# Two graph layers: the second layer's sent rows are loaded and halved in four of five pieces during the update of the last nodes

## The chip, the cores and the metric

The kernel runs on one core of a Trainium2 chip. The metric is the device time of one execution in microseconds (us), as the median of the runs; a profiled execution has a time of its own and a span, from its first to its last instruction. The core has five engines with a queue each: TensorE (PE, with PEld for loading its stationary operand), VectorE (DVE), ScalarE (ACT), GpSimd (POOL) and SyncE (SP), which issues most of the DMAs.

## The reference, cut to what matters

There are 3125 nodes of 256 numbers and 53125 directed edges. Four layers follow each other, each added to `x` behind a layer norm: an edge network with a node update, a mixture of four experts, a graph layer of two mean aggregations, and a feed-forward layer for the nodes with the highest weights. The graph layer is the one that matters here:

```python
def _sage_conv(x, src, tgt, W_l, b_l, W_r):
    msgs = x[src]
    agg = jax.ops.segment_sum(msgs, tgt, num_segments=n)
    deg = jax.ops.segment_sum(jnp.ones((src.shape[0],), x.dtype), tgt, num_segments=n)
    agg = agg / jnp.maximum(deg, 1.0)[:, None]
    return agg @ W_l + b_l + x @ W_r
h = jax.nn.relu(_sage_conv(x, src, tgt, W_l1, b1, W_r1))
logits = _sage_conv(h, src, tgt, W_l2, b2, W_r2)
```

## The kernel before, in words

The nodes are cut into 25 blocks of 128 (`NB`), and the blocks go through the node updates in pairs: block 24 alone first, then 0 and 1, up to 22 and 23.

*Dealing and edges.* The kernel first sorts the edges by source into buckets. The edge stage (`edges_by_bucket`, L776) then walks over 25 groups of buckets with five rounds each. POOL gathers rows of a table by indirect DMA (L807), VectorE adds (L845), ScalarE takes the relu (L850), and TensorE sums by source (L856). For each group it also counts the edges between every two nodes with one-hot matrices (L873 to L909) and writes the counts to `adj_h` in DRAM as f16. These tiles lie in the pool `bk`; `degs` and `hsb` of `close` (L859) hold what the group hands to the node update.

*Node updates.* They are generators that are advanced in small pieces between the steps of the edge stage. `first_part` is `update` (L583) and a layer norm; `second_part` is `experts` (L682), another layer norm and `sends` (L737). `update` loads `ux` on SyncE (L586), adds it to a matmul's result on VectorE (L619), and ends in L628. `experts` has two `sh` activations (L689 through `dense`, L579), four small expert networks (L709, L711), weights by L698 and L699, and adds the result to `x` at L734. `sends` writes a row block `zt` to `zres` in DRAM: its first half is what a node sends (times W_l1), its second what it keeps (times W_r1, plus the bias). The update tiles lie in the pool `upd`. All matmul results of the updates take turns in three PSUM banks (`ring(es, 3)`, L780).

When the last group is done, `all_pieces()` is called twice (L1015, L1016): the first call runs `first_part` of blocks 22 and 23 together with `second_part` of blocks 20 and 21 to their end, the second runs `second_part` of blocks 22 and 23.

*The graph layer.* `sums_of_few` (L1299) keeps the sent rows of all nodes on chip as `z1`, in two halves: the value rounded to the fast matmul type, and the rest. `halve` (L1307) makes them, the first on ScalarE (L1310), the second on VectorE (L1311). For each block of targets, `fetch` (L1315) loads the counts of two blocks as `two` (1600 KB), `widen` (L1324) turns one block of it into `slab`, its first nine parts on VectorE (L1328) and the other sixteen on ScalarE (L1329), `count` (L1332) adds up the degrees on VectorE, and 25 matmuls (L1402) sum into `padj`. The second sweep does the same with `z2`. The order of the work before the first sweep:

```python
fetch(0)
for k0 in range(0, NB, 5):
    v = z1[:, k0:k0 + 5, D:].bitcast(F32)
    nc.sync.dma_start(v, zres[k0 * P:(k0 + 5) * P, :D].rearrange("(k p) d -> p k d", p=P))
    if k0 == 0:
        widen(0)
        fetch(1), fetch(2)
    halve(z1, k0, v)
count(0)
```

A fetch of an odd block does nothing, since its pair is there already. Each engine works through its queue strictly in order. Within a stage that order is the one in which the kernel is written (a manual schedule), engine by engine, but the framework may draw work of a following stage forward where its inputs and its place in memory come free early. Before the change it does so with the first `two`, which stands behind `ux` and ahead of the last four stores of `zt`, and with slab 0, which is made among the L619 of blocks 22 and 23. The framework puts the tiles of pools into memory like a stack, from the left, or from the right where a pool says so, and makes the first user of a place wait for the last user of what lay there. The loads of the second layer's weights (`lr2`, L1191, and `b2`, L1192) and POOL's adds of `b2` to `x` (L1236) were drawn forward too, into the edge stage, one pair of adds with each pair of blocks.

Of the kernel before, what the change touches and what calls it, by code (L numbers as in the profile page):

```python
# [8 lines left out]
F32 = mybir.dt.float32  # L9
F16 = mybir.dt.float16  # L10
F32R = mybir.dt.float32r
I32 = mybir.dt.int32
AF = mybir.ActivationFunctionType
OP = mybir.AluOpType
AX = mybir.AxisListType

P = 128
N, E, D, HID = 3125, 53125, 256, 512
NB = -(-N // P)
# [31 lines left out]
def gnn_ffn_kernel(ctx: ExitStack, tc: tile.TileContext, a: dict, out: bass.AP):  # L51
    nc = tc.nc
# [6 lines left out]
    def ring(stack, bufs=8):  # L59
        rings.append(stack.enter_context(tc.tile_pool(name="psum", bufs=bufs, space=bass.MemoryType.PSUM)))  # L60
# [26 lines left out]
    def load(pool, name, shape, src, eng=None):  # L87
        t = pool.tile(shape, F32, name=name)
        (eng or queue[0]).dma_start(t, src)
        return t  # L90
# [7 lines left out]
    def row_bias(pool, name, b, n):  # L98
        return load(pool, name, [P, n], bass.AP(tensor=b.tensor, offset=b.offset, ap=[[0, P], [1, n]]))
# [57 lines left out]
    zres = dram.tile([NP, 2 * D], F32, name="zres")  # L157
# [4 lines left out]
    first = ExitStack()  # L162
# [353 lines left out]
    def rest_of(fast):  # L516

        rs, l0 = ExitStack(), ExitStack()
# [62 lines left out]
        st = {}  # L581
# [177 lines left out]
        def first_part(group, sums, got):  # L759

            yield from update(*group, sums)
            got.append((yield from normal(group, "xT1")))

        def second_part(group, got):

            yield from experts(*group, got[0])
            xT = yield from normal(group, "xT2")
            yield from sends(*group, xT)

        def finish_nodes(group, sums):  # L770
# [2 lines left out]
            yield  # L773
            yield from second_part(group, got)

        def edges_by_bucket():  # L776
            with tc.tile_pool(name="bk", bufs=2) as bp, tc.tile_pool(name="upd", bufs=2) as up, \
                    tc.tile_pool(name="pA", bufs=2, space=bass.MemoryType.PSUM) as pA, \
                    tc.tile_pool(name="pH", bufs=1, space=bass.MemoryType.PSUM) as pH, ExitStack() as es:
                ring(es, 3)  # L780
                st["up"] = up

# [138 lines left out]
                def pieces(n=1):  # L921
                    for _ in range(n):
                        next(parts[turn[0] > 2 and turn[0] % 2], None)
                        turn[0] += 1

                def all_pieces(pair=None, of=()):

                    pieces(99)
                    parts[1] = second_part(*going.pop()) if going else iter(())
                    parts[0] = iter(())  # L930
                    if pair:
                        got = []
                        parts[0] = first_part(pair, of, got)
                        going.append((pair, got))
                    turn[0] = 0


                def take(it, n=1):
                    for _ in range(n):
                        next(it, None)  # L940

                def step(i):
                    g, r = steps[i]
                    return units[g], r
# [14 lines left out]
                for hf, w in ((half0, W0), (half1, W1)):  # L959
                    left = NP - NBK * BN  # L960
# [17 lines left out]
                for i, (g, r) in enumerate(steps):  # L978
                    u, more = units[g], i + 1 < len(steps)
                    coming = []  # L980
                    if more:
                        v = step(i + 1)
# [25 lines left out]
                    if r == ROUNDS - 1:  # L1008
                        take(tally, 99)
                        tally = counts(units.pop(g))  # L1010
                        if g % UB == UB - 1 or g == order[0]:
                            k0 = g - g % UB
                            all_pieces((k0, g - k0 + 1), [sums.pop(k) for k in range(k0, g + 1)])
                take(tally, 99)
                all_pieces()  # L1015
                all_pieces()  # L1016
            rings.pop()

# [149 lines left out]
        if fast:  # L1168
            edges_by_bucket()
        else:  # L1170
            with ExitStack() as es:
                ring(es)
                with tc.tile_pool(name="keys", bufs=1) as kp:
                    edges_by_scatter(kp)
                st["up"] = es.enter_context(tc.tile_pool(name="upd", bufs=2))
                for k0, nb in PAIRS:
                    got = []
                    for k in range(k0, k0 + nb):
                        hs = st["up"].tile([P, HW], F32, name="h0")
                        nc.sync.dma_start(hs, hsum[k * P:(k + 1) * P, :])  # L1180
                        got.append((hs, None))
                    for _ in finish_nodes((k0, nb), got):
                        pass
            rings.pop()
        ring(rs)


        wl1 = rs.enter_context(tc.tile_pool(name="wl1", bufs=1, side="right"))
        lr2 = wl1.tile([P, 2, 2 * D], F32, name="lr2")
        for j, w in enumerate("lr"):  # L1190
            nc.sync.dma_start(lr2[:, :, j * D:(j + 1) * D], a[f"L1_gnn_W_{w}2"].rearrange("(k p) m -> p k m", p=P))  # L1191
        b2 = row_bias(wl1, "b2", a["L1_gnn_b2"], D)  # L1192
        l0.close()


        left, right = ExitStack(), ExitStack()
        cp = left.enter_context(tc.tile_pool(name="conv", bufs=1))
        slp = left.enter_context(tc.tile_pool(name="slab", bufs=2))
        rdeg = cp.tile([P, NB], F32, name="rdeg")
# [2 lines left out]
        def side_of(k):  # L1202
            return (half0, K0, k) if k < K0 else (half1, NB, k - K0)
# [95 lines left out]
        def sums_of_few():  # L1299
# [1 line left out]


            z2 = cp.tile([P, NB, 2 * D], F32R, name="z2")
            zp = right.enter_context(tc.tile_pool(name="z1p", bufs=2, side="right"))
            z1 = zp.tile([P, NB, 2 * D], F32R, name="z1", bufs=1)

            def halve(z, k, v):  # L1307

                first, rest = z[:, k:k + v.shape[1], :D], z[:, k:k + v.shape[1], D:]
                nc.scalar.activation(first, v, AF.Copy)  # L1310
                nc.vector.tensor_tensor(rest, v, first.bitcast(F32), op=OP.subtract)  # L1311

            pairs, slabs = {}, {}

            def fetch(k):  # L1315

                rows, end, o = side_of(k)
                if o % 2 == 0:
                    n = min(2, end - k) * P
                    two = slp.tile([P, NB, 2 * P], F16, name="two")  # L1320
                    nc.sync.dma_start(two[:, :, :n], rows[:, o * P:o * P + n].rearrange("(k p) c -> p k c", p=P))
                    pairs[k] = pairs[k + 1] = two, n

            def widen(k):  # L1324
                o = side_of(k)[2] % 2 * P
                slab = slp.tile([P, NB, P], F32R, name="slab")
                two = pairs[k][0]
                nc.vector.tensor_copy(slab[:, :9], two[:, :9, o:o + P])  # L1328
                nc.scalar.activation(slab[:, 9:], two[:, 9:, o:o + P], AF.Copy)  # L1329
                slabs[k] = slab  # L1330

            def count(k):  # L1332

                two, n = pairs[k]
                if side_of(k)[2] % 2:
                    return
                m = slp.tile([P, 12, 2 * P], F16, name="m12", bufs=1)
                with nc.allow_low_precision("whole numbers below 2048"):
                    nc.vector.tensor_tensor(m[:, :, :n], two[:, :12, :n], two[:, 12:24, :n], op=OP.add)
                    for w in (6, 3):  # L1340
                        nc.vector.tensor_tensor(m[:, :w, :n], m[:, :w, :n], m[:, w:2 * w, :n], op=OP.add)
                    nc.vector.tensor_tensor(m[:, 0, :n], m[:, 0, :n], m[:, 1, :n], op=OP.add)
                    nc.vector.tensor_tensor(m[:, 2, :n], m[:, 2, :n], two[:, 24, :n], op=OP.add)
                    deg = slp.tile([P, 2 * P], F16, name="degs")
                    nc.vector.tensor_tensor(deg[:, :n], m[:, 0, :n], m[:, 2, :n], op=OP.add)
                degs[k] = degs[k + 1] = deg
# [6 lines left out]

            degs = {}
            fetch(0)
            for k0 in range(0, NB, 5):
                v = z1[:, k0:k0 + 5, D:].bitcast(F32)
                nc.sync.dma_start(v, zres[k0 * P:(k0 + 5) * P, :D].rearrange("(k p) d -> p k d", p=P))  # L1358
                if k0 == 0:
                    widen(0)  # L1360
                    fetch(1), fetch(2)
                halve(z1, k0, v)
            count(0)

            todo = {}
# [1 line left out]
            for i in range(2 * NB + 1):  # L1367
                k, second = i % NB, i >= NB
# [38 lines left out]
        if fast:  # L1407
            with tc.manual_schedule():
                sums_of_few()
        else:  # L1410
            sums_of_any()
# [4 lines left out]
        with tc.tile_pool(name="ffn", bufs=2) as fp, tc.tile_pool(name="rank", bufs=1) as rp:  # L1416
# [8 lines left out]
            for k in range(NB):  # L1425
                w = wcol[:, k:k + 1]
# [13 lines left out]
            for k0, nb in GROUPS:  # L1440
# [5 lines left out]
                for i in range(nb):  # L1446
                    k = k0 + i
# [18 lines left out]
    with tc.If(ok > 0) as cmp:  # L1466
        rest_of(True)
    with cmp.Else():
        rest_of(False)
# [38 lines left out]
```

## Time and profile before

| | us |
|---|---|
| median of 3 runs | 2130.91 (2130.25 to 2131.38) |
| the profiled execution's own time | 2126.99 |
| its span | 2125.1 |

The span falls into stages, with TensorE's busy share of each from the trace:

| stage | from, to (us) | TensorE busy |
|---|---|---|
| dealing | 0 to 470 | 62% |
| edges, with the updates of blocks 24 and 0 to 21 | 470 to 1505 | 78% |
| rest of the updates of blocks 20 to 23 | 1505 to 1567 | 88% |
| from the last `zt` to the second block of the first sweep | 1567 to 1595 | 35% |
| first sweep | 1595 to 1791 | 100% |
| second sweep | 1791 to 1938 | 98% |
| last layer | 1938 to 2125 | 95% |

How to read a profile line: start and duration in us (of a group of equal instructions, merged), the engine, the line of the kernel, the operation, the tile written `<-` the tiles read, the shape, and in brackets how long the engine was idle before it and what released it. `SPq` is the queue of SyncE, which issues DMAs; its durations are those of issuing, not of the transfer. In the chain, a DMA's duration goes from its issue to its landing. The granted clock (`PEclk`) is the share of TensorE's full clock that was granted.

### The profile page before, as it was taken

What the parts mean: (1) busy time and instruction counts of PE and PEld (TensorE: products, weight loads), DVE (VectorE), ACT (ScalarE), POOL (GpSimd) and SP (SyncE); (2) the same over time, 40 slices, a digit from 0 to 9 for tenths busy, and PEclk for the clock granted to TensorE, in tenths of its full rate; (3) what the DMA queues carried; (4) which work ended last, traced back from release to release, by engine and by line L of the source; (5) the groups of instructions that cost most, each with busy time, mean ns of one, the idle gap of its engine ahead of it and who ended that gap; (6) DMA issues with size and microseconds to landing.
All of it is one profiled execution on the core that took longest, in us unless ns stands there. A gap on an engine that the chain in (4) does not pass through costs nothing. (4 is left out here: it accounts for less than half of the span.)

```text
span 2125.1 us, 25417 instructions
## 1 busy us (share of the span) xinstructions
PE 1681.3 (79%) x7515; PEld 1031.4 (49%) x7515; DVE 1488.9 (70%) x4174; ACT 942.0 (44%) x1695; POOL 983.9 (46%) x1044
## 2 busy tenths in 40 slices
PE   3666676661067898898899889889859999999998
PEld 1333232320034555465555555555537777886666
DVE  6888888883047878777777877778437675667960
ACT  1222222220047767666666676667333333443222
POOL 3677777777757655655565565564000000111011
PEclk9777777775579999999999999999989999999999
DMA  8332332321199777777776767774235545550010
GB/s 298 113 107 97 107 115 88 127 96 32 40 308 284 200 220 216 206 200 225 208 204 211 207 194 218 209 219 140 71 117 126 136 115 148 137 152 1 0 40 23
DMA packets 238444, 316.49 MB, mean 149 GB/s; under 512 B 34458, under 2 KB 168968, under 8 KB 237928
## 3 DMA queue, kind: packets, MB, share of 16 engines
q1 hardware_dynamic: 182216, 164.43, 25.8%
q0 software_dynamic: 52512, 142.96, 23.3%
q10 hardware_dynamic: 3568, 7.38, 1.0%
q8 instruction: 62, 1.02, 0.2%
q14 instruction: 86, 0.70, 0.1%
HBM read 229.71 MB, written 84.96 MB: 148 GB/s over the span
## 5 line engine op out<-in xcount | busy, mean ns | idle before, releaser
L807 POOL DMA_INDIRECT cb<-tab_b,goes_to x490 | 472.8, 965 | 372.7 <-issue 109.0
L438 POOL DMA_INDIRECT cbuf<-rt,to x416 | 410.5, 987 | 166.1 <-issue 99.8
L845 DVE TENSOR_TENSOR cb<-pa,cb 128x1024 f32<-128x1024 f32 x245 | 288.5, 1216 | 99.9 <-PE pa L840 64.3
L1402 PE MATMUL padj<-z,slab 128*128 128x512 f32 x1250 | 321.0, 409 | 15.9 <-DVE z L1311 15.8
L850 ACT ACTIVATE cb<-cb 128x1024 f32<-128x1024 f32 x245 | 254.8, 1051 | 56.5 <-DVE cb L845 55.8
L1402 PEld LDWEIGHTS padj<-z,slab 128*128 128x128 f32 x1250 | 232.2, 191 | 75.0 <-issue 23.0
L107 ACT ACTIVATE oT<-pt 64x512 fp32r<-64x512 f32 (+1 forms) x250 | 145.1, 580 | 176.8 <-PE pt L826 173.8
L900 PE MATMUL pn<-ob,oa 128*128 128x448 f16 (+1 forms) x692 | 160.3, 349 | 47.6 <-ACT cn L107 35.2
L130 POOL TENSOR_TENSOR x<-x,xn 128x256 f32<-128x256 f32 x25 | 24.5, 982 | 352.1 <-DVE xn L127 352.1
L840 PE MATMUL pa<-gives,oT 128*128 128x512 f32 x490 | 166.4, 462 | 21.9 <-ACT oT L107 10.2
L885 DVE TENSOR_SCALAR ob<-ids,rows 128x448 f16<-128x448 f16 (+1 forms) x490 | 165.0, 337 | 0.0
L881 DVE TENSOR_SCALAR oa<-ids,rows 128x128 f16<-128x128 f16 x692 | 164.9, 265 | 0.0
L343 PE MATMUL pp<-mw,xTa 128*128 128x512 f32 x200 | 138.6, 848 | 10.3 <-ACT xTa L107 10.3
L107 ACT ACTIVATE cn<-pn 128x352 f16<-128x352 f32 x196 | 97.3, 496 | 99.3 <-PE pn L900 88.9
L856 PE MATMUL ph<-cb,rows 128*32 128x512 f32 x980 | 140.1, 621 | 1.2 <-ACT cb L850 1.1
L900 PEld LDWEIGHTS <-oa 128*128 128x128 f16 x692 | 62.1, 99 | 160.2 <-issue 112.0
L331 PE MATMUL pt<-ident,xn 128*128 128x128 f32 x50 | 16.8, 438 | 133.8 <-DVE xn L326 133.8
L840 PEld LDWEIGHTS pa<-gives,oT 128*128 128x128 f32 x490 | 95.7, 205 | 53.5 <-ACT oT L107 14.9
L826 PE MATMUL pt<-ident_r,rows 128*64 128x128 f32 x490 | 52.4, 231 | 84.7 <-DMA rows<-cbuf 84.7
L1329 ACT ACTIVATE slab<-two 128x2048 fp32r<-128x2048 f16 x50 | 95.6, 1911 | 39.6 <-PE padj L1402 38.8
L107 ACT ACTIVATE total<-pk 1x98 f16<-1x98 f32 x103 | 24.5, 238 | 178.9 <-PE pk L404 178.8
L826 PEld LDWEIGHTS pt<-ident_r,rows 128*64 128x64 f32 x490 | 51.4, 143 | 104.5 <-issue 87.4
(242 smaller groups left out, 3029.5 us busy)
## 6 DMA issues: line engine op xcount, KB each, us to landing
two<-adj_h SPq DMA_DIRECT2D x24, 1600.0 KB
rows<-cbuf SPq DMA_DIRECT2D x25, 680.0 KB
gives<-tab_h SPq DMA_DIRECT2D x48, 256.0 KB
adj_h<-cn SPq DMA_DIRECT2D x100, 112.0 KB
adj_h<-cn SPq DMA_DIRECT2D x100, 88.0 KB
cb<-tab_b,goes_to POOLq DMA_INDIRECT x490, 4.3
cbuf<-rt,to POOLq DMA_INDIRECT x416, 2.2
cbuf<-empty ACTq DMA_DIRECT2D x4, 1632.0 KB
```

Source lines behind the costliest of these rows:

```text
L107: nc.scalar.activation(dst, src, AF.Copy)
L343: nc.tensor.matmul(pp, lhsT=xT[:, c, :], rhs=mw1[:, 2 * h + c, :], start=c == 0, stop=c == 1)
L438: one_of = nc.gpsimd.indirect_dma_start(out=cbuf[:], out_offset=bass.IndirectOffsetOnAxis(ap=to[:n, i:i + 1], axis=0), in_=rt[:n, i, :], i ...
L807: nc.gpsimd.indirect_dma_start(out=cb[:, j, :], out_offset=None, in_=tab_b[:], in_offset=bass.IndirectOffsetOnAxis(ap=u["to"][:, i:i + 1], ...
L840: nc.tensor.matmul(got[j // 2][:, j % 2, :], lhsT=oT[:, j, :], rhs=u["ag"][:, j, :], start=True, stop=True)
L845: nc.vector.tensor_tensor(cb[:, j:j + 2], pa, cb[:, j:j + 2], op=OP.add)
L850: nc.scalar.activation(h, h, AF.Relu)
L856: nc.tensor.matmul(u["ph"][j * BN:(j + 1) * BN, :], lhsT=u["rows"][:, GB * r + j, :BN].bitcast(F32), rhs=hs[j // 2][:, j % 2, :], start=r ...
L881: nc.vector.tensor_scalar(oa, ids[:, 1 + i * P:1 + (i + 1) * P], field[:, 0:1], None, op0=OP.is_equal)
L885: nc.vector.tensor_scalar(ob[:, :w], ids[:, 1:w + 1], field[:, 1:2], None, op0=OP.is_equal)
L900: nc.tensor.matmul(pn[:, :w], lhsT=u["oa"].pop((j, r, i)), rhs=u["ob"][j, r][:, :w], start=r == rs[0], stop=r == rs[-1])
L1402: nc.tensor.matmul(pa, lhsT=slab[:, c, :], rhs=(z2 if second else z1)[:, c, :], start=c == 0, stop=c == NB - 1)
```

## The change

Pool `bk` is opened after `upd` and closed when the last group's counts are done, ahead of the last two calls of `all_pieces`. At that place the weights of the second layer are loaded (`second_weights`), `z1` is placed, and four of its five pieces are loaded: the sent rows of blocks 0 to 19. After the first `all_pieces()`, `second_part` of the last pair is advanced in fives, and one of the four pieces is halved after each five. The fifth piece, blocks 20 to 24, is loaded and halved where all five were before. `halve` itself is the same, moved to an outer function.

```diff
--- before.py
+++ after.py
@@ -773,10 +773,27 @@
             yield
             yield from second_part(group, got)
 
+        right = ExitStack()
+
+        def halve(z, k, v):
+
+            first, rest = z[:, k:k + v.shape[1], :D], z[:, k:k + v.shape[1], D:]
+            nc.scalar.activation(first, v, AF.Copy)
+            nc.vector.tensor_tensor(rest, v, first.bitcast(F32), op=OP.subtract)
+
+        def second_weights():
+            wl1 = rs.enter_context(tc.tile_pool(name="wl1", bufs=1, side="right"))
+            st["lr2"] = lr2 = wl1.tile([P, 2, 2 * D], F32, name="lr2")
+            for j, w in enumerate("lr"):
+                nc.sync.dma_start(lr2[:, :, j * D:(j + 1) * D],
+                                  a[f"L1_gnn_W_{w}2"].rearrange("(k p) m -> p k m", p=P))
+            st["b2"] = row_bias(wl1, "b2", a["L1_gnn_b2"], D)
+
         def edges_by_bucket():
-            with tc.tile_pool(name="bk", bufs=2) as bp, tc.tile_pool(name="upd", bufs=2) as up, \
+            with tc.tile_pool(name="upd", bufs=2) as up, ExitStack() as of_edges, \
                     tc.tile_pool(name="pA", bufs=2, space=bass.MemoryType.PSUM) as pA, \
                     tc.tile_pool(name="pH", bufs=1, space=bass.MemoryType.PSUM) as pH, ExitStack() as es:
+                bp = of_edges.enter_context(tc.tile_pool(name="bk", bufs=2))
                 ring(es, 3)
                 st["up"] = up
 
@@ -1012,7 +1029,17 @@
                             k0 = g - g % UB
                             all_pieces((k0, g - k0 + 1), [sums.pop(k) for k in range(k0, g + 1)])
                 take(tally, 99)
+                of_edges.close()
+                second_weights()
+                st["z1"] = z1 = right.enter_context(tc.tile_pool(name="z1p", bufs=1, side="right")).tile(
+                    [P, NB, 2 * D], F32R, name="z1")
+                for k0 in range(0, NB - 5, 5):
+                    nc.sync.dma_start(z1[:, k0:k0 + 5, D:].bitcast(F32),
+                                      zres[k0 * P:(k0 + 5) * P, :D].rearrange("(k p) d -> p k d", p=P))
                 all_pieces()
+                for k0 in range(0, NB - 5, 5):
+                    pieces(5)
+                    halve(z1, k0, z1[:, k0:k0 + 5, D:].bitcast(F32))
                 all_pieces()
             rings.pop()
 
@@ -1185,15 +1212,13 @@
         ring(rs)
 
 
-        wl1 = rs.enter_context(tc.tile_pool(name="wl1", bufs=1, side="right"))
-        lr2 = wl1.tile([P, 2, 2 * D], F32, name="lr2")
-        for j, w in enumerate("lr"):
-            nc.sync.dma_start(lr2[:, :, j * D:(j + 1) * D], a[f"L1_gnn_W_{w}2"].rearrange("(k p) m -> p k m", p=P))
-        b2 = row_bias(wl1, "b2", a["L1_gnn_b2"], D)
+        if not fast:
+            second_weights()
+        lr2, b2 = st["lr2"], st["b2"]
         l0.close()
 
 
-        left, right = ExitStack(), ExitStack()
+        left = ExitStack()
         cp = left.enter_context(tc.tile_pool(name="conv", bufs=1))
         slp = left.enter_context(tc.tile_pool(name="slab", bufs=2))
         rdeg = cp.tile([P, NB], F32, name="rdeg")
@@ -1301,14 +1326,7 @@
 
 
             z2 = cp.tile([P, NB, 2 * D], F32R, name="z2")
-            zp = right.enter_context(tc.tile_pool(name="z1p", bufs=2, side="right"))
-            z1 = zp.tile([P, NB, 2 * D], F32R, name="z1", bufs=1)
-
-            def halve(z, k, v):
-
-                first, rest = z[:, k:k + v.shape[1], :D], z[:, k:k + v.shape[1], D:]
-                nc.scalar.activation(first, v, AF.Copy)
-                nc.vector.tensor_tensor(rest, v, first.bitcast(F32), op=OP.subtract)
+            z1 = st["z1"]
 
             pairs, slabs = {}, {}
 
@@ -1353,13 +1371,11 @@
 
             degs = {}
             fetch(0)
-            for k0 in range(0, NB, 5):
-                v = z1[:, k0:k0 + 5, D:].bitcast(F32)
-                nc.sync.dma_start(v, zres[k0 * P:(k0 + 5) * P, :D].rearrange("(k p) d -> p k d", p=P))
-                if k0 == 0:
-                    widen(0)
-                    fetch(1), fetch(2)
-                halve(z1, k0, v)
+            v = z1[:, NB - 5:, D:].bitcast(F32)
+            nc.sync.dma_start(v, zres[(NB - 5) * P:, :D].rearrange("(k p) d -> p k d", p=P))
+            widen(0)
+            fetch(1), fetch(2)
+            halve(z1, NB - 5, v)
             count(0)
 
             todo = {}
```

In the resulting order of the engines' queues, SyncE issues the three loads of weights and the four pieces ahead of `ux` of blocks 22 and 23 (L586), and the first `two` after the last store of `zt`. On ScalarE and VectorE the four halvings stand among the instructions of `experts` for blocks 22 and 23. TensorE's order is the same. POOL's first twenty adds of `b2` stand together behind the last gathers.

## The prediction

> **What bounds the kernel now.** I first read the page's chain of work that ended last. From 1595.08 us on it is TensorE nearly without a break (L1402, L1232, then the last layer), so whatever moves the start of that stretch moves the end by as much. The chain over 1500 to 1600 us shows what sets that start (start, us, what):
>
> ```profile
> 1566.55 0.43 DVE zt L745
> ...
> 1567.00 2.03 DMA zres<-zt
> ...
> 1577.50 9.35 DMA z<-zres
> ...
> 1586.87 1.28 ACT z L1310
> ...
> 1588.17 1.49 DVE z L1311
> 1589.66 1.68 DVE m L1339
> ...
> 1593.76 1.27 DVE slab L1328
> ...
> 1595.08 4.30 PE padj L1402 x12
> ```
>
> The last zt row is ready at Z = 1566.98; block 1 of the first sweep starts 28.1 us later. Of these, 21.2 go until the fifth piece of z1 is on VectorE (1588.17), and 6.9 to its halving, `count` and the copy of slab 1. This end is what the change attacks. The SyncE queue says why the pieces come late (start, us, engine, line):
>
> ```profile
> 1505.09 1.28 SPq L586 DMA_DIRECT2D ux<-own  x1
> 1512.54 0.38 SPq L1321 DMA_DIRECT2D two<-adj_h  x1
> 1540.99 26.33 SPq L747 DMA_DIRECT2D zres<-zt  x4
> 1569.19 0.37 SPq L1358 DMA_DIRECT2D z<-zres  x1
> 1569.61 0.52 SPq L1321 DMA_DIRECT2D two<-adj_h  x1
> 1570.18 8.84 SPq L1358 DMA_DIRECT2D z<-zres  x4
> ```
>
> It serves in order: ux, the first `two`, four stores, and only then five pieces, with a second 1600 KB `two` between them. ScalarE took the pieces up at 1573.47, 1581.22, 1583.10, 1584.97 and 1586.87: one after the other, 1.9 us each for 640 KB, at 345 to 351 GB/s.
>
> The third view is the ux consumer in the node updates. These are VectorE's and TensorE's lines:
>
> ```profile
> 1513.26 0.42 DVE L619 TENSOR_TENSOR uT<-pd,ux 128x256 f32<-128x256 f32 x1 [0.79 <-PE pd L618]
> ```
> ```profile
> 1515.65 1.03 PE L578 MATMUL pd<-xT,ew 128*128 128x256 f32 x4
> ...
> 1522.42 1.78 PE L628 MATMUL pupd<-uw,uT 128*128 128x256 f32 x7 [0.57 <-DVE uT L619]
> ```
>
> ux was issued at 1505.09 and never waited for. The matmuls at 1515.65 need the PSUM bank that this first L619 frees (ring of three). Last, the granted clock (window, length, busy us, clock, DMA share, GB/s) falls when TensorE idles:
>
> ```profile
> 1585.00:1587.00 2.00, 2.00 (x6) 1.52 (x5) 1.62 (x2) 1.38 (x2) 0.00 (x0) 0.50 0.82 260
> 1587.00:1589.00 2.00, 2.00 (x8) 1.58 (x8) 1.60 (x2) 2.00 (x2) 0.00 (x0) 0.85 0.00 0
> ...
> 1595.00:1597.00 2.00, 1.92 (x6) 1.53 (x6) 1.80 (x7) 1.91 (x1) 0.00 (x0) 0.50 0.28 44
> ```
>
> **Part 1, the four early pieces: a new wait for ux.** In the changed program's order SyncE issues lr2 (two), b2, four pieces, and only then ux. The first piece lies over the edge tiles (cb, hsb, degs, oa, ob), so it waits for the last reader of degs, the second L611 pair, as the first `two` does today: issue at 1512.54, not 1505. ux waits for nothing itself, but stands behind it. Data flowed at full rate about 1.9 us after an issue (`two` at 1512.54: 190 GB/s by 1514 to 1515, 338 after). Four pieces and ux are 4x0.655 + 0.524 = 3.15 MB; at 348 GB/s 9.0 us, so ux lands at 1512.54 + 1.9 + 9.0 + 0.4 = 1523.9. L619 goes from 1513.26 to 1523.9. VectorE holds everything behind it (all L619, L699, L630, the norms), TensorE stops before the matmuls of 1515.65 and ScalarE behind both. They resume at 1523.9 + 0.45 = 1524.35.
>
> From there TensorE's queue up to L628 is 6.2 us of work (1515.65 to 1521.85), at first at half clock: TensorE has stood 8.7 us. In the row above it got its full clock back 3.3 us after it became busy at 1584.07, so about 1.6 us are lost. L628 starts at 1524.35 + 6.2 + 1.6 = 1532.15 instead of 1522.42: **+9.75**. (Before lost 0.57 there, since slab 0's copy stood ahead of the last L619; that goes.) Bounds: ux not queued behind the data would land at about 1516.2 + 4 = 1520.2 (today some 4 us from issue to last byte), -3.7; at the 290 GB/s of `two` it comes 1.9 later.
>
> **Part 2, the four halvings in the last pair's experts.** Each is 1.27 us ScalarE and 1.49 VectorE; the pieces have landed 20 us before. The order gives their places. The first ScalarE copy stands ahead of the two `sh` activations at 1544.48: `sh` comes 1.35 later, TensorE's next matmuls 1.2. The second and third stand ahead of L711, where ScalarE idled 0.74 each: they add 0.2 or less. The fourth follows the last L711, in a 5 us idle. On VectorE the first three fit the waits ahead of both L699 (3.77 and 2.61 idle); the fourth stands between L734 and the statistics at 1558.00, on the path: 1.45. Sum 1.45 + 1.45 = **+2.9**; 0 if all hide, 4x(1.27 + 1.49) = 11.0 if none does. With 0.1 for a colder clock at L742, Z moves by 9.75 + 2.9 + 0.1 = **+12.75**.
>
> **Part 3, from Z to block 1.** The first `two` no longer goes early: it now lies over the update tiles, zt among them, and stands behind the fourth store. Issue at Z + 2.05 (store) + 0.15 = Z + 2.2; landing, by its row (1512.54 to 1520.56), 8.0 later, Z + 10.2. The fifth piece follows it by 1.9, Z + 12.1. ScalarE copies its part of slab 0 (1.91 from Z + 10.25), then halves (1.27); VectorE takes the fifth piece at Z + 13.5 instead of Z + 21.2: **-7.7**. The 6.9 us behind it stay. Block 0 hides: its first nine matmuls need only VectorE's part (Z + 11.6), 22 of them take some 7 us with the cold start, and `degs` comes at Z + 19.1. TensorE is then busy shortly before block 1, whose first twelve matmuls took 4.30 at the clock of 0.50 above; warm, at the 3.58 for fifteen of the later blocks, 2.87: **-1.4**. The second `two` and res come 5.8 + 0.9 after the fifth piece, Z + 18.8, and are needed at Z + 20.9: hidden by 2 us; without cover it is their lateness.
>
> A rule would make this sum otherwise. The Trainium skill, "DMA: Bandwidth & Descriptors", "Anatomy of one DMA", gives a fit of about 2.0 us plus bytes/436e3 (for the software path; SBUF side). By it ux lands after 2.0 + 7.2 us, 2.1 sooner, and `two` after 5.8 instead of 8.0: the total below would be about -1. The rows of this very queue are 348 and 290 GB/s; I take them.
>
> **Part 4, what costs nothing.** lr2 and b2 leave the middle of the edge stage, and 18 of POOL's adds of b2 (L1236) with them: each pair was followed by 2.5 to 4.4 us of idle POOL until ScalarE's hsb, so a shorter burst releases no gather; that stage is 88% TensorE. Bound: the one VectorE wait for a gather after 816 us, 3.0. The 20 adds (0.74 each) then run from about 1508 to 1524, ahead of POOL's L728, needed at 1542. The other edits rename or reorder pools.
>
> **Sum.** +12.75 - 7.7 - 1.4 = +3.65, say +3.7. Against the profiled execution's 2126.99 us (span 2125.1) that is 2130.7; the median of the runs is 2130.91, so I predict **2134.6**. A difference within 0.2% (4.3 us) is about what a measurement of this kernel can't tell from none.
>
> **Rivals.**
> - *ux is not held up* (the engines share it with the pieces, or the pieces go earlier). For it: 16 engines. Against: today's pieces landed strictly one after another. Then +9.75 goes: 2130.9 + 2.9 + 0.1 - 9.1 = 2124.8, faster. Half held, at 1520.2: about 2131.
> - *The halvings hold the expert chain*, slower: each of ScalarE's four copies delays an activation that TensorE waits for, 4x1.27 + 1.49 = 6.6 instead of 2.9: 2138.3. It decides once L628 to the last zt grows by over 5 us. For: strict order, short idles (0.74). Against: the three idles above.
> - *The change doesn't do what it says*: pieces that land after their halving. They land by 1522, the first halving comes at about 1554; 2% at most.
>
> **Chances.** Mine, 2132 to 2137.5: 55%. The halvings, late pieces or a longer ux wait: 27%. Partly or not held up: 18%, the smaller part of it below 2126.6. The upper part of my own case is beyond +4.3. So faster 0.11, same 0.41, slower 0.48; range 2127 to 2139.5.
>
> **What would show it.** ux landing near 1524 with an L619 that waits for DMA, and a TensorE hole of 8 to 9 us from 1515.6; a clock of 0.50 behind it; the last zt near 1580; the first `two` issued 2.2 behind it; block 1 near 1600 at full clock. If L619 doesn't wait, the first step is wrong and the kernel is faster; if Z comes after 1583, the second is.

## The result and the profile after

The changed kernel takes 2136.65 us (median of 20 runs, 2131.11 to 2140.29), the kernel before 2130.47 us in the same runs (20, 2126.66 to 2135.51). The ratio is 1.0025, with a 95% interval of 1.0017 to 1.0034: 5.3 us slower (3.6 to 7.2); the two medians lie 6.2 apart. Predicted were 3.7 us more.

The profiled execution of after took 2140.28 us (span 2138.5), 3.6 above its median; that of before 3.5 below its own. By the spans the change would cost 13.4 us. The rows say where the surplus lies: the last adj_h store of the edge stage is issued at 1504.72 before and at 1512.53 after, 7.8 us later. The eight runs of the experiments spread by 14 us there (1661.86 to 1676.27 on their chip), so two profiled executions don't tell how much of the 7.8 is the change's, if any. So from here on I count from this store, S. The first transposition that stands among block 1's matmuls (L1224 before, L1249 after; it turns block 0's result, and is called block 1's transpose below) stands for the end, since what follows it takes 525.9 us in both. It comes at S + 94.50 before and S + 100.02 after: 5.5 us, in line with the 5.3 of the ratio.

Of the chain of work that ended last, the lines that answer to before's (start, us, what):

```profile
1591.72 9.30 DMA z<-zres
...
1601.07 7.88 PE padj L1418 x22
...
1608.97 3.74 PE padj L1418 x15
```

One round of loads is left between the store of the last zt row (ready at Z = 1589.14) and TensorE. The name in the first line (`z<-zres`) misleads: the first padj waits for VectorE's slab copy, and the fifth piece landed by chance last (1601.01, the copy ended at 1600.97); the program needs that piece 20 matmuls later. The last line is three matmuls of block 0 and twelve of block 1, which now took 0.25 each, warm (at full clock). SyncE's queue (start, us):

```profile
1521.56 2.21 SPq L1037 DMA_DIRECT2D z<-zres  x4
1523.81 1.51 SPq L586 DMA_DIRECT2D ux<-own  x1
...
1591.29 0.37 SPq L1339 DMA_DIRECT2D two<-adj_h  x1
```

ux goes out behind four pieces, S + 11.3 instead of S + 0.4; the first `two` goes out behind the stores. VectorE and TensorE in the node updates (the bracket is idle time, and what ended it):

```profile
1518.25 0.70 DVE L671 TENSOR_TENSOR equal<-equal,prior 128x32 f32<-128x32 f32 x1
1518.99 0.65 DVE L672 TENSOR_TENSOR ahead<-ahead,equal 128x32 f32<-128x32 f32 x1
...
1520.90 0.59 DVE L611 SCALAR_TENSOR_TENSOR aT<-degs,mb,pagg 128x128 f32<-128x128 f32 x2
1532.82 0.76 DVE L619 TENSOR_TENSOR uT<-pd,ux 128x256 f32<-128x256 f32 x2 [11.33 <-DMA ux<-own]
```
```profile
1533.30 2.08 PE L578 MATMUL pd<-xT,ew 128*128 128x256 f32 x4 [8.47 <-DVE uT L619]
...
1541.82 1.89 PE L628 MATMUL pupd<-uw,uT 128*128 128x256 f32 x8
```

L619 waits for ux, as predicted, and TensorE stands for 8.47 us. The first two lines of VectorE were not predicted. They belong to the gate, a chain of short instructions (L651 to L679) ahead of the second L611 pair. In the kernel before they read:

```profile
1510.44 0.19 DVE L671 TENSOR_TENSOR equal<-equal,prior 128x32 f32<-128x32 f32 x1
1510.66 0.19 DVE L672 TENSOR_TENSOR ahead<-ahead,equal 128x32 f32<-128x32 f32 x1
```

Beside them POOL now does this:

```profile
1518.18 13.66 POOL L1261 TENSOR_TENSOR x<-x,b 128x256 f32<-128x256 f32 x20 [33.63 <-DMA b<-in_L_gnn_b_dram]
```

And the clock when TensorE resumes (window, length, busy us of PE, PEld, DVE, ACT and POOL, clock, DMA share, GB/s):

```profile
1533.00:1535.00 2.00, 1.70 (x4) 1.43 (x5) 0.58 (x2) 0.99 (x2) 0.00 (x0) 0.50 0.00 0
1535.00:1537.00 2.00, 2.00 (x5) 1.09 (x4) 0.00 (x0) 0.47 (x1) 0.00 (x0) 0.50 0.00 0
1537.00:1539.00 2.00, 2.00 (x10) 1.10 (x10) 0.42 (x1) 0.77 (x2) 0.00 (x0) 0.66 0.00 0
```

Half speed for 5 us of work (0.66 over the last 2 us is 1.36 us of it), not for 3.3. The halvings show in two waits of TensorE, for `sh` and for the last norm. Before, there was no wait at `sh`, and this one at the norm:

```profile
1560.11 1.01 PE L138 MATMUL pt<-ident,xn 128*128 128x128 f32 x4 [2.64 <-DVE xn L127]
```

After:

```profile
1565.24 1.13 PE L578 MATMUL pd<-sh,sw 128*128 128x256 f32 x4 [0.93 <-ACT sh L579]
...
1581.88 1.11 PE L138 MATMUL pt<-ident,xn 128*128 128x128 f32 x4 [4.05 <-DVE xn L127]
```

From the gate's matmuls (L638) to these transposes it takes 18.47 us before and 21.22 after: 1.20 more up to the first L709, 0.02 from there to the first L730, 1.53 from there on. Behind Z, VectorE:

```profile
1599.62 1.35 DVE L1346 CAST slab<-two 128x1152 fp32r<-128x1152 f16 x1 [10.48 <-DMA two<-adj_h]
1602.73 1.49 DVE L782 TENSOR_TENSOR z<-z 128x1280 fp32r<-128x1280 f32 x1 [1.76 <-ACT z L781]
```

The fifth piece's halving starts at Z + 13.6 (before Z + 21.2).

### The profile page after: what moved, and what is told of

It reads as the page before. It is cut to its first block, busy times and chain, and to the rows that moved or that the text cites. A ratio compares the mean times of both kernels' runs of the same rounds, so it can differ in the third digit from the quotient of the medians.

```text
span 2138.5 us, 25426 instructions
## 1 busy us (share of the span) xinstructions
PE 1681.4 (79%) x7515; PEld 1030.2 (48%) x7515; DVE 1491.5 (70%) x4174; ACT 939.8 (44%) x1695; POOL 982.6 (46%) x1044
## 3 DMA queue, kind: packets, MB, share of 16 engines
q8 instruction: 62, 1.02, 0.2%
```

## Experiments

They ran on another chip, where the kernel before takes 2287.7 to 2289.0 us; ratios are to that. (The table's rows before and after are the first chip's.) The surplus over the first chip lies ahead of S, and the runs scatter by 30 us, so a ratio tells 2 parts in 1000 at best. The stage in question agrees with the first chip's rows to a tenth of a microsecond where nothing was changed, so the distances in the profile decide:

| kernel | second L611 pair, S + | first L628, S + | L628 to Z | Z to block 1's transpose | transpose, S + | ratio to before (95%) |
|---|---|---|---|---|---|---|
| before | 7.15 | 17.70 | 44.55 | 32.25 | 94.50 | 1 |
| after | 8.37 | 29.29 | 47.32 | 23.41 | 100.02 | 1.0025 (1.0017 to 1.0034) |
| e1, ux first | 7.16 | 16.97 | 48.92 | 23.41 | 89.30 | 0.9964 (0.9942 to 0.9985) |
| e2, b2 early | 7.16 | 28.29 | 47.46 | 23.25 | 99.00 | 1.0035 (1.0018 to 1.0052) |
| e3, halved late | 8.82 | 29.55 | 43.98 | 23.22 | 96.75 | 1.0032 (1.0011 to 1.0052) |
| e7, ux in the middle | 8.35 | 25.36 | 47.12 | 23.36 | 95.84 | 1.0017 (0.9996 to 1.0038) |
| e5, all three | 7.15 | 16.97 | 43.97 | 23.14 | 84.08 | 0.9946 (0.9924 to 0.9967) |
| e10, spread | 7.16 | 16.97 | 44.17 | 23.20 | 84.34 | 0.9953 (0.9933 to 0.9973) |
| e8, `two` early | 8.34 | 29.43 | 47.40 | 18.92 | 95.75 | 1.0015 (0.9992 to 1.0038) |
| e9, all of it | 7.16 | 16.98 | 45.58 | 14.49 | 77.05 | 0.9883 (0.9843 to 0.9922) |

**e1, ux ahead of the pieces.**

```diff
                 take(tally, 99)
+                pieces()
                 of_edges.close()
```

> The changed kernel with one thing moved: ux of the last pair is issued ahead of the second layer's weights and the four z pieces, as in the kernel before. My theory (ux stands behind 2.6 MB of pieces, and behind the wait of the first piece): ux lands long before L619, L619 waits for no DMA, the hole of 8.5 us on TensorE and the half-speed clock behind it go, L628 comes 10 to 11 us sooner; the whole is 10 us faster than the changed kernel and about 5 us faster than the one before (ratio 0.9976). What stays: the halvings (+2.9), POOL's adds beside VectorE's gate chain (+1.2), and the shorter way from the last zt row to block 1 (-9.1). Rival (the loss is made by the halvings and by the first two that comes late, and the wait for ux is covered by something else that is just as late): less than 3 us faster than the changed kernel, still at or above the kernel before.

VectorE's first L619, and POOL:

```profile
1676.42 0.42 DVE L619 TENSOR_TENSOR uT<-pd,ux 128x256 f32<-128x256 f32 x1 [0.79 <-PE pd L618]
...
1686.85 0.42 DVE L630 TENSOR_TENSOR x<-pupd,x 128x256 f32<-128x256 f32 x1 [2.44 <-PE pupd L628]
```
```profile
1676.14 13.72 POOL L1262 TENSOR_TENSOR x<-x,b 128x256 f32<-128x256 f32 x20 [36.24 <-DMA b<-in_L_gnn_b_dram]
```

No L619 waits for a DMA, L628 comes 12.3 us sooner than in the changed kernel, the transpose 10.7 sooner and 5.2 sooner than before. The wait for ux is the loss; the rival falls. Two details differ from the expectation. b2 lands later here, so POOL's adds start behind the gate chain: L671 and L672 are at 0.19. And L628 to Z takes 1.6 longer than in the changed kernel; that is TensorE's clock ahead of the first zt pair:

```profile
1696.85:1698.85 2.00, 1.21 (x5) 0.72 (x5) 0.90 (x3) 0.53 (x3) 1.23 (x2) 0.56 0.00 0
1698.85:1700.85 2.00, 2.00 (x3) 0.97 (x4) 0.00 (x0) 0.28 (x1) 0.28 (x1) 0.50 0.03 8
1700.85:1702.85 2.00, 2.00 (x3) 0.78 (x3) 0.00 (x0) 0.28 (x1) 0.00 (x0) 0.50 0.00 0
1702.85:1704.85 2.00, 2.00 (x5) 0.73 (x4) 0.42 (x1) 0.11 (x1) 0.00 (x0) 0.73 0.30 110
```

Counting 2 us times (1 - clock) / 0.5 in each row, that is 6.8 us at half speed; the same sum at the same place gives 3.4 in e7, in e2 and in after.

**e2, b2 loaded ahead of the edge stage.**

```diff
                 st["up"] = up
+                second_weights()
...
                 of_edges.close()
-                second_weights()
```

> The changed kernel, but lr2 and b2 are loaded ahead of the edge stage, so that POOL's adds of b2 can run before the last pair's gate. My theory (POOL's adds slow VectorE's short instructions beside them, 0.70 us for L671 and 0.65 for L672 instead of 0.19): both are back at about 0.19, the second L611 pair and with it the first piece and ux come 1.2 us sooner, and the kernel is 1.2 us faster than the changed one, 4 us above the one before (ratio 1.0019); a size at the edge of what five rounds tell, so the durations of the instructions decide. Rival (they are slow for another cause: the clock, or a write of PSUM beside them): 0.6 to 0.7 as in the changed kernel, and no gain.

```profile
1673.53 0.19 DVE L671 TENSOR_TENSOR equal<-equal,prior 128x32 f32<-128x32 f32 x1
1673.76 0.19 DVE L672 TENSOR_TENSOR ahead<-ahead,equal 128x32 f32<-128x32 f32 x1
```

With POOL's adds elsewhere both are back, the second L611 pair is 1.21 sooner and the transpose 1.02. The ratio can't show so little. That it is the adds is shown: the edit moves the loads of lr2 and b2 as well, but in e1 these ran beside L671 (353 GB/s from 1672 to 1674), which stayed at 0.19. Which instructions the adds slow is seen with e1, too: there the same 20 run beside L619 and L630, which keep their 0.42. Those read one operand from PSUM and one from SBUF; L671 and L672 read two from SBUF. In the changed kernel L676 and L679, with two from SBUF, took 0.33 and 0.25 instead of 0.17, and L673, L677 and L678, with one, no longer than before. The Trainium skill, "SBUF — State Buffer", "Who interferes with whom", has this rule: a VectorE instruction with two SBUF inputs contends with a GpSimd one that reads SBUF; one with at most one SBUF input does not, outside the modes that take both port pairs. These rows agree with it (0.70 and 0.65 against 0.42 unchanged).

**e3, the four pieces halved behind Z.**

```diff
                 all_pieces()
-                for k0 in range(0, NB - 5, 5):
-                    pieces(5)
-                    halve(...)
                 all_pieces()
+                for k0 in range(0, NB - 5, 5):
+                    halve(...)
```

> The changed kernel with the four early pieces still loaded early, but halved only behind the last zt rows, while ScalarE and VectorE wait for the first two (10 us). My theory (two of the eight halving instructions stand on the experts' path and cost 1.45 us each): from L628 to the last zt row it takes 2.7 us less than in the changed kernel, the halvings fit ahead of the slab copies, block 1 starts at the same distance behind the last zt row, and the kernel is 2.7 us faster than the changed one, about 2.5 above the one before (ratio 1.0012). Rival 1 (halvings among the experts fill idle time only): no change. Rival 2 (the eight instructions delay the slab copies): up to 2 us slower.

VectorE behind Z:

```profile
1743.50 5.70 DVE L782 TENSOR_TENSOR z<-z 128x1280 fp32r<-128x1280 f32 x4 [0.73 <-ACT z L781]
1753.03 1.35 DVE L1345 CAST slab<-two 128x1152 fp32r<-128x1152 f16 x1 [3.84 <-DMA two<-adj_h]
```

L628 to Z falls by 3.3 and Z to the transpose stays: four halvings fit where VectorE waits for `two`, and 3.84 us of that wait are left. Part of the 3.3 is the clock (3.4 us at half speed around the last zt pair here, 6.8 in after), so the halvings' own price is better read from after against before: 2.8, with 10.2 us at half speed on this way in both. Rival 2 falls; rival 1 as well by the rows. The ratio, expected at 1.0012, came out at 1.0032 (the rows' 2.25 us make 1.0010): its interval (from 1.0011) just holds the expectation, and doesn't tell it from the changed kernel's 1.0025.

**e7, ux between the second and the third piece.**

```diff
                 for k0 in range(0, NB - 5, 5):
+                    if k0 == 10:
+                        pieces()
                     nc.sync.dma_start(z1[...], zres[...])
```

> The changed kernel with ux issued between the second and the third z piece. Both still stand behind the first piece's wait. If it is the data in front that holds ux up (the queue's transfers go one after the other at about 350 GB/s), ux lands 7.6 us behind the first piece's issue instead of 11.2, and L619, L628 and the end come 3.6 to 4 us sooner than in the changed kernel (about 1.5 above the one before, ratio 1.0007). If the DMA engines share the four pieces and ux, or if the wait ahead of the first piece alone is what costs, ux lands where it did, and the time is that of the changed kernel (1.0025).

```profile
1684.67 0.76 DVE L619 TENSOR_TENSOR uT<-pd,ux 128x256 f32<-128x256 f32 x2 [7.58 <-DMA ux<-own]
```

The first piece was issued at 1677.16: L619 starts 7.5 behind it instead of 11.3. The transpose comes 4.2 sooner. So the queue moves one transfer after the other: two pieces less are 1.31 MB, 3.8 us at 348 GB/s, and 3.75 were measured. It is the data in front that holds ux up.

**e5, the three edits together** (the diffs of e1, e2 and e3).

> The changed kernel with three things put back: ux ahead of the pieces, lr2 and b2 ahead of the edge stage, and the four halvings behind the last zt rows. Of the change only the early loads stay. If the losses add up as the single edits gave them (L628 12.3 us sooner, the way from L628 to the last zt row 3.3 us shorter, the way from there to block 1 as in the changed kernel), the first transpose of block 1 comes 84 to 84.5 us behind the last adj_h store, 10 us sooner than in the kernel before (94.5) and 15.5 sooner than in the changed one; ratio to before about 0.9955. Rival (the edits cover one another, so that they don't add): less than 8 us sooner than before.

84.08: they add up. What is left of the change, the early loads alone, is worth 10.4 us against before, a ratio of 0.9954; the medians of all runs (2277.35 and 2287.72) make 0.9955.

**e10, e5 with the halvings spread.**

```diff
-                for k0 in range(0, NB - 5, 5):
-                    pieces(5)
+                for k0, n in ((0, 4), (5, 2), (10, 6), (15, 99)):
+                    for _ in range(n):
+                        next(parts[1], None)
                     halve(...)
-                all_pieces()
```

> As the kernel with all three put back, but three halvings stay among the experts and norms: ahead of L699 of the first pair of experts, between its L711s, and ahead of the last zt copies; the fourth is behind the last zt row. My theory (in the changed kernel only the first ScalarE copy, ahead of the sh activations, and the fourth VectorE halving, ahead of the statistics, were on the path; the two in the middle filled idle time): from L628 to the last zt row it takes the 44.0 us of the kernel that halves late, within 0.5, and the time is the same. Rival (every halving costs about a quarter of the 3.3 us): 1.6 to 2.5 us more on that way.

44.17 against 43.97, both with 6.8 us at half speed: the three that stay among the nodes' work cost next to nothing there. In the changed kernel the calls of `pieces` take turns between two generators, one of which is empty by then, so "in fives" moves `second_part` on by one, three, two and three steps, and halvings stand behind steps 1, 4, 6 and 9. Here they stand behind steps 4, 6 and 12 and at the end: the changed kernel's two in the middle stay, and its first and last leave their places. With TensorE's rows above, two of its eight instructions were on the path, ScalarE's first and VectorE's last; the others filled idle time.

**e8, the first `two` early.**

```diff
+                twos = rs.enter_context(tc.tile_pool(name="twos", bufs=2, side="right"))
                 st["z1"] = z1 = ...
...
                 all_pieces()
+                st["two0"] = twos.tile([P, NB, 2 * P], F16, name="two")
+                nc.sync.dma_start(st["two0"], half0[:, :2 * P].rearrange("(k p) c -> p k c", p=P))
...
-            fetch(0)
+            pairs[0] = pairs[1] = st["two0"], 2 * P
```

> The changed kernel with the pool of the adjacency pairs laid where the edge stage's tiles were, so that the first two need not wait for the update's tiles: it is issued behind the stores of the next-to-last pair, some 28 us ahead of the last zt row. ux stays behind the pieces. My theory (behind the last zt row it is now the landing of the first two, 10.4 us, that sets slab 0, the fifth piece, the count and with it block 1): the fifth piece is issued first and lands about 6.2 us behind the last zt row instead of 11.9, degs comes at 13.2 instead of 19.2, the first transpose of block 1 comes 17.6 us behind the last zt row instead of 23.4; the whole is 5.8 us faster than the changed kernel, level with the one before (ratio 1.000). Rival (VectorE's work behind the last zt row or TensorE's cold clock holds it): less than 2 us gained.

```profile
1742.27 6.91 PE L1422 MATMUL padj<-z,slab 128*128 128x512 f32 x22 [4.47 <-DVE slab L1350]
1752.24 0.18 PE L1373 MATMUL pdg<-ids,degs 128*128 128x1 f16 x1 [3.06 <-DVE degs L1367]
1752.28 5.49 PE L1422 MATMUL padj<-z,slab 128*128 128x512 f32 x15
```

The way behind Z shrinks by 4.5, not 5.8. Z is 1738.69: degs ended at Z + 13.5, about as expected, so the landing of `two` was what set the end. The missing 1.3 is in the last line: TensorE stood 3.06 us for degs, its clock fell to 0.50, and the fifteen matmuls that took 3.74 in the chain above took 5.49. An earlier release gave part of itself back through the clock.

**e9, all of it.** The edits of e5 (halvings as in e10) and e8, the second `two` early as well, and behind Z another order:

```diff
             widen(0)
-            fetch(1), fetch(2)
-            halve(z1, NB - 5, v)
             count(0)
+            widen(1)
+            halve(z1, NB - 5, v)
```

> All of it together: ux ahead of the pieces, lr2 and b2 ahead of the edge stage, both first adjacency pairs loaded early in a pool of their own, the halvings spread as in the run above, and behind the last zt row the order slab 0, count, slab 1, fifth piece's halving. Expected: L628 17 us behind the last adj_h store, 44.3 from there to the last zt row, and 15.9 to the first transpose of block 1 (slab 0 from 2.1, when the last store is read, count to 7.5, slab 1 to 8.9, fifth piece to 10.4, five more matmuls and fifteen of block 1): 77.2 us, 17.3 us sooner than in the kernel before; ratio about 0.9925. If the gain behind the last zt row can't be had (as the rival above says), 84 us, like the kernel with three things put back.

```profile
1730.81 6.45 PE L1428 MATMUL padj<-z,slab 128*128 128x512 f32 x20 [4.47 <-DVE slab L1354]
1737.53 0.73 PE L1428 MATMUL padj<-z,slab 128*128 128x512 f32 x2 [0.27 <-DVE z L782]
...
1738.14 3.73 PE L1428 MATMUL padj<-z,slab 128*128 128x512 f32 x15
```

TensorE starts 3.6 us behind Z and stops once more, for 0.27. 77.05 against 77.2: 17.4 us sooner than before. This is the fastest of all, 0.9883 of before (0.9843 to 0.9922, from six executions). The rows account for 19 us of it, with 1.8 behind the transpose, or 0.9916, which the interval holds; the medians make 0.9903.

## Why the prediction was right, and where its sizes were off

Predicted and measured, in us of the profiled executions, by its own terms:

| term | predicted | measured |
|---|---|---|
| ux behind the pieces (L628) | +9.75 | +11.59 |
| halvings and a colder clock (L628 to Z) | +3.0 | +2.77 |
| Z to block 1, with the warm clock | -9.1 | -8.84 |
| sum | +3.65 | +5.52 |

- **Part 1** has the right mechanism (e1 takes the whole wait away, e7 part of it). ux landed 11.17 behind the first piece's issue; 11.36 was the estimate. The fit of the page weighed there would have had it at 9.2: the queue's own rows, 348 and 290 GB/s, were the better guide. Two things make the 1.84 that the term lacks, less the 0.19 by which ux landed faster. The first piece went out at S + 9.03, not at S + 7.82: 1.21, POOL's adds. And from the landing to L628 it took 9.09, not 8.25: 0.84, the clock, for which I had taken 3.3 us of half speed from one row (its 0.85 makes 3.5) where it was 5.
- **Part 4** is wrong in one item, and this is the step that failed: of the 20 adds of b2 I asked only whether they delay POOL's own next work, "ahead of POOL's L728", and set them at nothing. They delay VectorE's gate chain, on which the release of the first piece hangs, by 1.2 (e2). Its bound is misread: two waits of VectorE for a gather stand behind 816 us (930.04 and 1455.00, 3.0 each), not one. The rest of that part is not contradicted: of the interval of 3.6 to 7.2, 5.5 us behind S leave at most 1.7 for the edge stage.
- **Part 2** is right in size and place: `sh` and the statistics paid 1.20 and 1.53, the middle ones 0.02 (e3 and e10 agree). It is 0.2 too high.
- **Part 3** is right: `two` issued at Z + 2.15, landed at about Z + 10.4, the fifth piece on VectorE at Z + 13.6 against 13.5, block 1 warm. e8 shows that the landing of `two`, which the change made late itself, took away 4.5 us of what the early pieces could have given.

Of the rivals, "ux is not held up" is excluded by e1 and e7. "The halvings hold the expert chain" is excluded by the 2.8 us. The change did what it says: no halving waited for its piece, and ux, which stood behind all four, was in at 1532.73, 31 us ahead of the first one (1563.56). The result came out on the slower side of my forecast by Part 1's two terms, the issue 1.21 later that Part 4 had put at nothing and the 0.84 of the clock.

## What to carry to other kernels

- A load moved to an earlier place in a queue that serves in order pushes every load behind it back, and takes its own wait with it. Ask for each transfer behind it who needs it first; here one line that let the small, urgent ux go ahead turned 5 us lost into 5 us won.
- A buffer's place in memory is part of the schedule: the early pieces took the room of the edge stage's tiles, and the adjacency pair, moved onto tiles still in use, lost its head start. Laying it elsewhere gave 4.5 us.
- When idle filler moves on one engine, look at the other engine's instructions beside it, too, and at which operands they read.

## What the runs showed of the hardware

**POOL beside VectorE.** 20 adds of 128x256 on POOL made a short product and a short sum of VectorE over two SBUF operands (128x32) 0.70 and 0.65 us long instead of 0.19 (after), and left sums with a PSUM operand at 0.42 (e1).

**The clock comes back in steps.** By the sum used in e1, each stretch at half speed around the two zt pairs lasted 3.4 or 6.8 us, or there was none; nothing between. For the first pair: none in e5 and e10, 3.4 in after, e2, e3, e7 and e8, 6.8 in before, e1 and e9. For the second: 3.4 in before, e3 and e9, 6.8 in the others. That fits what the Trainium skill says in "TensorE: Matmul & The Clock Gate", "Part 1: The HAM clock gate (the "warmup" mystery)": activity is judged over a free-running window of about 3.4 us. What a stop costs therefore depends on when it falls in the window, and a figure from one row, such as my 3.3 us, can be off by up to a window. From L628 to Z, e1 has 3.4 us more at half speed than the changed kernel and takes 1.6 longer; e9 has 3.4 more than e10 and takes 1.4 longer, which is about what it lacks to the 44.3 expected.
